# Spreading edge weights instead of messages, and running the last tiles' experts ahead of their gates: a fused graph layer on one Trainium2 core

## Chip, cores and metric

The kernel runs on 1 core of one Trainium2 chip. The metric is device time in microseconds (us) of that core, from start to end of one launch; lower is better.

## What is computed

A node layer over x of 6250 rows by 256: a graph attention over 200,000 edges, a linear attention, a sum, a norm, and then a mixture of four experts whose gates come from a second, small graph attention over 131,072 edges (edges to nodes past 6250 fall away). The change lies in this last part:

```python
h = (x_flat @ W_gat).reshape(M, HEADS, NUM_EXPERTS)              # 4 heads x 4 values a node
e = leaky_relu(a_src[src] + a_dst[dst], negative_slope=0.2)
alpha = softmax of e over the edges that share a dst
agg = segment_sum(h[src] * alpha[:, :, None], dst) + b_gat
scores = layernorm(agg).reshape(M, HEADS, NUM_EXPERTS).mean(1)
topk_s, topk_i = top_k(scores, 2);  w = softmax(topk_s)
for ei in range(4):
    g = where(topk_i == ei, w, 0.0).sum(-1)
    hh = gelu(x @ W1[ei] + b1[ei])
    out = out + g[..., None] * (hh @ W2[ei] + b2[ei])
```

The four experts can be computed without the gates; only the weighting and the sum need them.

## The kernel before

Nodes lie in 49 tiles of 128 (the last has 106). The first stage (first graph attention, linear attention, sorting of the second edge list) ends at about 2200 us of the profiled span, and the change leaves its work as it is, but for a few tiny operations in the check that sets `bad_2`. What matters starts there.

**Second edges.** The sorted edges are cut into 98 groups (`NGR`) of `G2` = 8 chunks of 128 edges, with some two groups to a tile of nodes. A group touches at most `W2` = 2 neighbouring tiles; `ohq` (128x8x2) says to which of the two an edge belongs. For each group, class `SecondEdges` has these steps, each a method:

- `gather` (L1303): 8 indirect DMAs on GpSimd (POOL), one for each chunk, which fetch each edge's source row from `htab` in DRAM. Six buffers, issued three groups ahead.
- `load` (L1319, SP queue), `one_hot_t` (L1332), `one_hot` (L1324): the one-hot matrices of the edges.
- `terms` (L1345, PE), `select` (L1353, L1357): the destination's factors, masked by `ohq`, summed to `pw`.
- `weights` (L1361, L1362): `pr = pw * gathered factors`, `wp = max`, 4 weights an edge. The first operation of DVE that needs the gather.
- `messages` (L1365 to L1377): `msg = values * wp` (160 elements a partition), split into three bf16 parts `m3` by four operations, and then `mq = m3 * ohq`, 960 bf16 elements, which puts each message into the columns of its tile and zeros into the other's.
- `add` (L1385 on PE, L1389, L1391 on DVE): one-hot times `mq`, summed over the group, added to `acc2`.

The intermediate `pw`, `wp` and `msg` lie in PSUM, in the tile `dv`.

**Gates.** `gates(w, lo, hi)` turns `acc2` of finished tiles into the gate of each expert: 33 short dependent steps on DVE (with one tanh on ACT). The list `GATES` says in which group's turn the gates of which tiles start; a step costs one `next()`, and up to `HOPS` = 7 are written out in each of three places of a group's turn.

**Experts.** `expert_steps` makes one list of 458 steps: for a pair (expert, block of `TT` = 4 tiles) a begin, 4 hidden steps (L1404 on PE, gelu on ACT at L1409) and one output step for each tile (L1422, L1424 on PE, then a `sink` on DVE). Experts 0 and 1 come first, ungated; they go to DRAM (`keep`, `early`). Then come experts 2 and 3, block by block (`total`): the sink of expert 2 multiplies the two early outputs, loaded back by `load_early`, by their gates and adds the node's row `kx` (L1497, L1498); both sinks add their own gated output straight from PSUM (L1499); the sink of expert 3 sends the tile out (L1501). So an output of experts 2 and 3 can't be used before its tile's gates are known.

**The order of the work** is written out by hand: one loop over the groups issues the methods above, and `experts(part)` writes out as many expert steps as a straight line from group 0 to group 98 asks for, but the last `REST` = 30, which come after the gates of tiles 44 to 48:

```python
experts_upto(FIRST + (3 * g + part) * (len(e_steps) - REST - FIRST) // (3 * NGR))
...
for _ in gates(w, GATED, NT):
    pass
experts_upto(len(e_steps))
```

Each engine works through its own instructions in order, and waits at the first one that isn't ready. A conditional block behind the loop (`bad != 0`) recomputes everything for edge lists that don't fit these assumptions.

Of the kernel before, what the change touches and what calls it, by code (L numbers as in the profile page):

```python
# [9 lines left out]
F32 = mybir.dt.float32  # L10
BF16 = mybir.dt.bfloat16
# [3 lines left out]
OP = mybir.AluOpType  # L15
AX = mybir.AxisListType
# [4 lines left out]
P = 128  # L21
# [11 lines left out]
G2 = 8  # L33
# [16 lines left out]


GB = 8
GATES = [(t, min(t + GB, 40), 2 * min(t + GB, 40) + 3) for t in range(0, 40, GB)] + [(40, 44, 91)]
GATED = 44


def rows(t):
    return min(P, N - t * P)
# [3 lines left out]
def gps_layer(ctx: ExitStack, tc: tile.TileContext, a: dict, out: bass.AP):  # L62
# [1157 lines left out]
    with tc.tile_pool(name="d_k", bufs=1) as dk:  # L1220
# [64 lines left out]
        class SecondEdges:  # L1285
# [4 lines left out]
            def __init__(self, w, gp, ps, dv, idx, dl, q, rows, eds, narrow=False):  # L1290
                self.w, self.gp, self.ps, self.eds, self.narrow = w, gp, ps, eds, narrow
                self.idx, self.dl, self.q, self.rows = idx, dl, q, rows
                self.lane = dv[:, 0:P]
                at = P
                for name, f in (("pw", 8), ("wp", 4), ("msg", HW)):
                    setattr(self, name, dv[:, at : at + G2 * f].rearrange("p (c f) -> p c f", f=f))
                    at += G2 * f

            def gather(self):
                self.gt = self.gp.tile([P, G2, HW + 8], F32, name="gt")  # L1300
# [49 lines left out]
            def select(self):  # L1350

                es = self.w.tile([P, G2, W2 * 3, 8], F32, name="e_sel", bufs=1)
                V.tensor_mul(  # L1353
                    es.rearrange("p c (q s) f -> p c q (s f)", q=W2), self.ed,
                    self.ohq[:, :, :, None].to_broadcast([P, G2, W2, 24]),
                )
                V.tensor_reduce(self.pw, es.rearrange("p c k f -> p c f k"), AX.X, OP.add)  # L1357

            def weights(self):
                pr = self.w.tile([P, G2, 8], F32, name="pr", bufs=1)  # L1360
                V.tensor_mul(pr, self.pw, self.gt[:, :, HW:])  # L1361
                V.tensor_max(self.wp, pr[:, :, 0:4], pr[:, :, 4:8])  # L1362

            def messages(self):
                V.tensor_mul(  # L1365
                    self.msg.rearrange("p c (h d) -> p c h d", h=4),
                    self.gt[:, :, 0:HW].rearrange("p c (h d) -> p c h d", h=4),
                    self.wp.unsqueeze(3).to_broadcast([P, G2, 4, 5]),
                )

                m3 = self.w.tile([P, G2, 3, HW], BF16, name="m3")
                V.tensor_copy(m3[:, :, 0], self.msg)
                V.tensor_sub(self.msg, self.msg, m3[:, :, 0])  # L1373
                V.tensor_copy(m3[:, :, 1], self.msg)
                V.tensor_sub(m3[:, :, 2], self.msg, m3[:, :, 1])
                self.mq = self.w.tile([P, G2, W2, 3 * HW], BF16, name="mq")
                V.tensor_mul(  # L1377
                    self.mq, m3.rearrange("p c s f -> p c (s f)")[:, :, None, :].to_broadcast([P, G2, W2, 3 * HW]),
                    self.ohq[:, :, :, None].to_broadcast([P, G2, W2, 3 * HW]),
                )  # L1380

            def add(self):
                ag = self.ps.tile([P, W2 * 3 * HW], F32, name="ag")
                for c in range(G2):
                    T.matmul(  # L1385
                        ag, self.oh[:, c], self.mq[:, c].rearrange("p q f -> p (q f)"), start=(c == 0), stop=(c == G2 - 1)
                    )
                part_ = self.w.tile([P, W2, HW], F32, name="ag3", bufs=1)
                V.tensor_reduce(part_, ag.rearrange("p (q s f) -> p q f s", q=W2, s=3), AX.X, OP.add)  # L1389
                at = acc2[:, ds(self.t, W2), :]  # L1390
                V.tensor_add(at, at, part_)  # L1391

# [87 lines left out]

        gated_to = 0

        def total(e, t0):


            def begin():
                if e == EARLY:
                    if t0 == 0:
                        load_early(0)
                    load_early(t0 + TT)  # L1490

            def sink(t, yo):
                assert t < gated_to
                n = rows(t)
                y = held[t0][:n, :, t - t0]
                if e == EARLY:
                    V.scalar_tensor_tensor(y[:, 0], y[:, 0], gate[:n, t, 0:1], kx[:n, t], op0=OP.mult, op1=OP.add)  # L1497
                    V.scalar_tensor_tensor(y[:, 0], y[:, 1], gate[:n, t, 1:2], y[:, 0], op0=OP.mult, op1=OP.add)  # L1498
                V.scalar_tensor_tensor(y[:, 0], yo[:n], gate[:n, t, e : e + 1], y[:, 0], op0=OP.mult, op1=OP.add)  # L1499
                if e == 3:  # L1500
                    SP.dma_start(out[t * P : t * P + n, :], y[:, 0])  # L1501

            return begin, sink

        def gates(w, lo, hi):

# [100 lines left out]
            yield  # L1607

        late = [(e, t0) for t0 in blocks for e in range(EARLY, 4)]
        e_steps = expert_steps([(e, t0) for e in range(EARLY) for t0 in blocks] + late, lambda e, t0: (keep if e < EARLY else total)(e, t0))  # L1610
        e_done = 0

        def experts_upto(k):
            nonlocal e_done
            for st_ in e_steps[e_done:k]:
                st_()
            e_done = max(e_done, k)

        with tc.tile_pool(name="g2_w", bufs=2) as w, tc.tile_pool(name="g2_g", bufs=6) as gp, tc.tile_pool(
# [9 lines left out]
                groups.append(SecondEdges(w, gp, ps, dv, src_2[:, cols], dl_2[:, cols], q_2[:, cols],  # L1629
                                          rows_2[g * G2 * P : (g + 1) * G2 * P, :], 2, g < NARROW))  # L1630
            AHEAD = 4
            REST = 30
            FIRST = 14
            in_turn = []
            HOPS = 7
            at_ = lambda i: groups[i].load()
            at_(0)
# [1 line left out]
            for g in range(-3, NGR + 1):  # L1639
                def at(i, stage):  # L1640
                    if 0 <= i < NGR:
                        getattr(groups[i], stage)()
                def experts(part):
                    if g < 0:
                        return experts_upto((3 * (g + 3) + part) * FIRST // 9)
                    for _ in range(HOPS):
                        if in_turn and next(in_turn[0], 0) == 0:
                            in_turn.pop(0)
                    experts_upto(FIRST + (3 * g + part) * (len(e_steps) - REST - FIRST) // (3 * NGR))
                if g == -3:  # L1650
                    for i in range(AHEAD):
                        at(i, "gather")
                elif g > 0:
                    at(g + AHEAD - 1, "gather")
                i = g + 3
                if 0 <= i < NGR and i % TL == 0:
                    _, ts_ = nc.values_load_multi_w_load_instructions(
                        t0_2[0:1, i : min(i + TL, NGR)], engines=(ENG.Activation, ENG.DVE), min_val=0, max_val=NT,
                        skip_runtime_bounds_check_because="the tiles are clamped",
                    )  # L1660
                    for j, t in enumerate(ts_):
                        groups[i + j].t = t
                in_turn += [gates(w, lo, hi) for lo, hi, g_ in GATES if g_ == g]
# [24 lines left out]
                experts(3)  # L1688
            for _ in gates(w, GATED, NT):
                pass  # L1690
            experts_upto(len(e_steps))
        with tc.If(bad != 0):

            own_edges()
# [26 lines left out]
            with tc.tile_pool(name="l_w", bufs=1) as w:  # L1721
                for lo in range(0, NT, GB):
                    for _ in gates(w, lo, min(lo + GB, NT)):
                        pass
            for st_ in expert_steps(late, total):
                st_()

# [27 lines left out]
```

## Time and profile before

| | |
|---|---|
| median of 3 runs | 3260.65 us (3256.18 to 3268.05) |
| the profiled execution's own time | 3258.8 us |
| its span, first to last instruction | 3257.0 us |
| granted clock of TensorE, mean | 0.857 |
| busy share PE, DVE, POOL, ACT | 72%, 75%, 72%, 15% |
| first and last gather of the second edges issued | 2200.41 us, 3202.68 us |
| last expert output leaves DVE | 3249.8 us |

A line of a group reads: line, engine, operation, output<-inputs, shapes and count, then busy time in all and the mean ns of one, then the idle time of the engine just before them and what ended most of it. A line of the timeline reads: start, duration, engine, line, operation, and in brackets the idle time of the engine before it. "issue" is time in which the engine waited for nothing that the profile shows. Instructions of one engine overlap at their ends, so the start of the next is a better measure of what one costs than its duration.

### The profile page before, as it was taken

To read this page: it belongs to the slowest core of one execution; us is meant where nothing else is said; L and a number is where in the kernel's file an instruction comes from. 1 tells how busy PE (TensorE), PEld (TensorE's weight loads), DVE (VectorE), ACT (ScalarE), POOL (GpSimd) and SP (SyncE) were. 2 spreads that over 40 slices of the span, in tenths; PEclk is the share of its full clock that TensorE was granted. 3 is DMA by queue.
4 is the path that set the end of the run, shared out by engine and by line. 5 is a ranking of instruction groups with operands and counts; after the bars stand their busy time and mean duration, and the time that the engine had idled before them with its cause. 6 is when DMAs were issued, how large, how long until landed. Compare 5 with 4: busy or idle time off the path is not lost. (4 is left out here: it accounts for less than half of the span.)

```text
span 3257.0 us, 36396 instructions
## 1 busy us (share of the span) xinstructions
PE 2334.0 (72%) x10899; PEld 1699.4 (52%) x10900; DVE 2439.4 (75%) x6337; ACT 480.6 (15%) x1266; POOL 2344.4 (72%) x2436
## 2 busy tenths in 40 slices
PE   7677778865666574665665666658777877888888
PEld 5555666654455453554544545445455545555555
DVE  7587767788888887886886878667676766777775
ACT  3200111111111111111111111013111111111111
POOL 2577777777777777777777777757777777777772
PEclk9788888987888887787888878779998998999989
DMA  6544444445555555555555555534223223333321
GB/s 202 155 135 135 136 129 127 137 134 145 150 139 151 143 137 140 138 141 143 141 153 142 147 140 142 138 92 101 61 62 78 60 57 92 81 76 80 78 51 37
DMA packets 248273, 384.90 MB, mean 118 GB/s; under 512 B 73414, under 2 KB 156246, under 8 KB 248057
## 3 DMA queue, kind: packets, MB, share of 16 engines
q0 software_dynamic: 103296, 230.96, 28.9%
q1 hardware_dynamic: 142857, 150.87, 15.4%
q8 instruction: 91, 1.49, 0.2%
q14 instruction: 125, 1.02, 0.1%
q10 hardware_dynamic: 1904, 0.56, 0.1%
HBM read 345.44 MB, written 36.74 MB: 117 GB/s over the span
## 5 line engine op out<-in xcount | busy, mean ns | idle before, releaser
L774 POOL DMA_INDIRECT gt<-ztab,src_c x1612 | 1551.2, 962 | 528.1 <-issue 424.7
L842 PE MATMUL ag<-gt,oh 128*128 128x260 f32 x3224 | 980.1, 461 | 348.3 <-DVE gt L833 347.0
L842 PEld LDWEIGHTS ag<-gt,oh 128*128 128x128 f32 x3224 | 732.6, 234 | 516.0 <-DVE gt L833 375.9
L1303 POOL DMA_INDIRECT gt<-htab,src x784 | 764.6, 975 | 262.5 <-issue 210.0
L833 DVE TENSOR_TENSOR gt<-gt,dv 128x1040 f32<-128x1040 f32 x403 | 488.8, 1223 | 0.2 <-DVE src L409 0.2
L1424 PE MATMUL yo<-w,hT 128*128 128x256 f32 x1568 | 420.8, 411 | 15.8 <-DVE ys L1467 15.8
L1404 PE MATMUL hp<-xy,w 128*128 128x512 f32 (+1 forms) x832 | 407.2, 612 | 8.6 <-ACT hT L1409 4.5
L1424 PEld LDWEIGHTS yo<-w,hT 128*128 128x128 f32 x1568 | 303.5, 203 | 96.1 <-issue 26.3
L208 DVE TENSOR_TENSOR src_d<-gt,most 128x32 f32<-128x32 f32 x204 | 38.6, 189 | 355.6 <-DMA gt<-ztab,src_c 344.3
L868 PE MATMUL m<-wqkv,xy 128*128 128x256 f32 (+1 forms) x784 | 235.8, 436 | 88.8 <-DVE kmax L879 43.6
L798 DVE TENSOR_TENSOR oh<-dv,dl_c 128x1024 f32<-128x1024 f32 x202 | 243.9, 1207 | 0.0
L868 PEld LDWEIGHTS m<-wqkv,xy 128*128 128x128 f32 (+1 forms) x784 | 160.7, 215 | 125.1 <-DVE kmax L879 49.6
L1404 PEld LDWEIGHTS hp<-xy,w 128*128 128x128 f32 x832 | 159.9, 205 | 112.4 <-issue 98.3
L1409 ACT ACTIVATE hT<-hp,b 128x512 f32<-128x512 f32 (+1 forms) x208 | 132.8, 660 | 517.6 <-PE hp L1404 294.9
L209 ACT ACTIVATE src_f<-src_d,shift_c 128x32 f32<-128x32 f32 x202 | 64.9, 321 | 928.2 <-DVE src_d L208 836.3
L1361 DVE TENSOR_TENSOR pr<-dv,gt 128x64 f32<-128x64 f32 x98 | 21.9, 223 | 227.0 <-DMA gt<-htab,src 219.5
L1385 PE MATMUL ag<-mq,oh 128*128 128x120 bf16 x784 | 66.3, 236 | 150.4 <-DVE mq L1377 141.0
L813 PE MATMUL ed<-pw,ohT 128*128 128x24 bf16 x1612 | 72.1, 175 | 125.5 <-DVE ohT L807 111.1
L373 DVE MAX8 src<-dl 128x8 f32<-128x1024 f32 x128 | 156.0, 1219 | 0.4 <-issue 0.4
L1385 PEld LDWEIGHTS <-oh 128*128 128x128 bf16 x784 | 51.6, 107 | 198.5 <-DVE mq L1377 176.6
L375 DVE MATCH_REPLACE8 dl<-src,dl 128x1024 f32<-128x1024 f32 x127 | 153.4, 1208 | 0.0
L813 PEld LDWEIGHTS <-ohT 128*128 128x128 bf16 x1612 | 64.0, 98 | 165.4 <-DVE ohT L807 134.3
(350 smaller groups left out, 2695.0 us busy)
## 6 DMA issues: line engine op xcount, KB each, us to landing
br<-rows SPq DMA_DIRECT2D x299, 256.0 KB
gt<-ztab,src_c POOLq DMA_INDIRECT x1612
gt<-htab,src POOLq DMA_INDIRECT x784
early<-ys SPq DMA_DIRECT2D x24, 512.0 KB
ys<-early SPq DMA_DIRECT2D x24, 512.0 KB
ztab<-zt SPq DMA_DIRECT2D x48, 132.0 KB
row<-in_x_dram SPq DMA_DIRECT2D x48, 128.0 KB
out_dram<-ys SPq DMA_DIRECT2D x48, 128.0 KB
```

Of the source, the lines that this page charges most:

```text
L373: V.max(out=srtf[:, 8 * i : 8 * i + 8], in_=keyf)
L375: V.match_replace(out=keyf, in_to_replace=srtf[:, 8 * i : 8 * i + 8], in_values=keyf, imm_value=0.0)
L774: G.indirect_dma_start(out=self.gt[:, c, :], out_offset=None, in_=ztab[:, :], in_offset=bass.IndirectOffsetOnAxis(ap=self.idx[:, c : c + 1 ...
L798: V.tensor_tensor(self.oh[:, :n], self.dv[:, None, :P].to_broadcast([P, n, P]), self.dl[:, :, None].to_broadcast([P, n, P]), op=OP.is_equal,)
L813: T.matmul(self.ed[:, c, :], self.ohT[:, c * P : (c + 1) * P], pw3[:, ds(self.tiles[c], 1), :].rearrange("p a b -> p (a b)"), start=True, ...
L833: V.tensor_mul(gz, gz, self.wp[:, c0:c1].unsqueeze(3).to_broadcast([P, c1 - c0, 4, 65]))
L842: T.matmul(sums[t], self.oh[:, c], self.gt[:, c, 0:ZW], start=(s0 + c == 0 or chunk_tile[s0 + c - 1] != t), stop=last,)
L868: T.matmul(out_, xy[:, t, j, :n], wqkv[:, j, c0 : c0 + D], start=(j == 0), stop=(j == 1))
L1303: G.indirect_dma_start(out=self.gt[:, c, : tab.shape[1]], out_offset=None, in_=tab[:, :], in_offset=bass.IndirectOffsetOnAxis(ap=self.idx[ ...
L1404: T.matmul(hp[:, :m], wts[e][0][:, c, j * P : (j + 1) * P], xy[:, t0 : t0 + nt, c] if m == nt * P else xy[:, t0, c, :m], start=(c == 0), s ...
L1409: S.activation(h[:, :m], hp[:, :m], AF.Gelu, bias=b1[:, e, j : j + 1])
L1424: T.matmul(yo[:n], hT[j][:, o : o + n], wts[e][1][:, j, :], start=(j == 0 and e < EARLY), stop=(j == 3))
```

## The change

1. `weights` multiplies the 4 weights of an edge by `ohq` into `wq` (8 chunks x 2 tiles x 4 heads = 64 elements); `messages` multiplies the gathered values by `wq` and so makes messages for both tiles at once (320 elements). The split into three bf16 parts runs over these 320 and writes `mq` directly; the product of 960 and the buffer `m3` are gone. `pw` and `wp` move from PSUM to SBUF.
2. For tiles 36 to 48 experts 2 and 3 run ungated, like experts 0 and 1: their outputs are copied by ACT (`hold`) into rows of `kx` that belong to tiles 0 to 25 and aren't needed any more. `total_held` puts gates and the four outputs together later.
3. `REST` is now a number of groups: all expert steps are written out by group 95. The gates are cut finer at the end (`GATED` = 46), and two steps of `total_held` run in each of the three places of a group's turn when no gate step is pending.
4. The first 26 tiles of `kx` are saved to DRAM (`rows_d`) by two DMAs in groups 4 and 8, for the conditional block.

```diff
-GATES = [(t, min(t + GB, 40), 2 * min(t + GB, 40) + 3) for t in range(0, 40, GB)] + [(40, 44, 91)]
-GATED = 44
+GATES = [(t0, t1, 2 * t1 + 3) for t0, t1 in [(0, 8), (8, 16), (16, 24), (24, 32), (32, 36), (36, 40), (40, 44), (44, 46)]]
+GATED = 46
+HELD = 36
...
+                self.pw = self.w.tile([P, G2, 8], F32, name="pw")
                 V.tensor_reduce(self.pw, es.rearrange("p c k f -> p c f k"), AX.X, OP.add)
             def weights(self):
...
-                V.tensor_max(self.wp, pr[:, :, 0:4], pr[:, :, 4:8])
+                wp = self.w.tile([P, G2, 4], F32, name="wp", bufs=1)
+                V.tensor_max(wp, pr[:, :, 0:4], pr[:, :, 4:8])
+                V.tensor_mul(
+                    self.wq, wp[:, :, None, :].to_broadcast([P, G2, W2, 4]),
+                    self.ohq[:, :, :, None].to_broadcast([P, G2, W2, 4]),
+                )
             def messages(self):
                 V.tensor_mul(
-                    self.msg.rearrange("p c (h d) -> p c h d", h=4),
-                    self.gt[:, :, 0:HW].rearrange("p c (h d) -> p c h d", h=4),
-                    self.wp.unsqueeze(3).to_broadcast([P, G2, 4, 5]),
+                    self.msg.rearrange("p c (q h d) -> p c q h d", q=W2, h=4),
+                    self.gt[:, :, 0:HW].rearrange("p c (h d) -> p c h d", h=4)[:, :, None].to_broadcast([P, G2, W2, 4, 5]),
+                    self.wq.unsqueeze(4).to_broadcast([P, G2, W2, 4, 5]),
                 )
-                m3 = self.w.tile([P, G2, 3, HW], BF16, name="m3")
-                V.tensor_copy(m3[:, :, 0], self.msg)
-                V.tensor_sub(self.msg, self.msg, m3[:, :, 0])
-                V.tensor_copy(m3[:, :, 1], self.msg)
-                V.tensor_sub(m3[:, :, 2], self.msg, m3[:, :, 1])
-                self.mq = self.w.tile([P, G2, W2, 3 * HW], BF16, name="mq")
-                V.tensor_mul(
-                    self.mq, m3.rearrange("p c s f -> p c (s f)")[:, :, None, :].to_broadcast([P, G2, W2, 3 * HW]),
-                    self.ohq[:, :, :, None].to_broadcast([P, G2, W2, 3 * HW]),
-                )
+                self.mq = self.w.tile([P, G2, 3, W2 * HW], BF16, name="mq")
+                V.tensor_copy(self.mq[:, :, 0], self.msg)
+                V.tensor_sub(self.msg, self.msg, self.mq[:, :, 0])
+                V.tensor_copy(self.mq[:, :, 1], self.msg)
+                V.tensor_sub(self.mq[:, :, 2], self.msg, self.mq[:, :, 1])
...
+        def hold(e, t0):
+            def sink(t, yo):
+                S.copy(kx[: rows(t), (e - EARLY) * NH + t - HELD], yo[: rows(t)])
+            return (lambda: None), sink
+        def add_early(t):
+            y = held[t - t % TT][:n, :, t % TT]
+            V.scalar_tensor_tensor(y[:, 0], y[:, 0], gate[:n, t, 0:1], kx[:n, t], op0=OP.mult, op1=OP.add)
+            yield
+            V.scalar_tensor_tensor(y[:, 0], y[:, 1], gate[:n, t, 1:2], y[:, 0], op0=OP.mult, op1=OP.add)
+            yield
+        def add_late(t, e, yo):
+            V.scalar_tensor_tensor(y, yo[:n], gate[:n, t, e : e + 1], y, op0=OP.mult, op1=OP.add)
+            if e == 3:
+                SP.dma_start(out[t * P : t * P + n, :], y)
...
+        def total_held(lo, hi):
+            for t in range(lo, hi):
+                if t % TT == 0:
+                    load_early(t)
+                yield from add_early(t)
+                for e in range(EARLY, 4):
+                    add_late(t, e, kx[:, (e - EARLY) * NH + t - HELD])
+                    yield
...
-            REST = 30
+            REST = 3
...
+                    for _ in range(2):
+                        if in_turn_2 and not in_turn and next(in_turn_2[0], 0) == 0:
+                            in_turn_2.pop(0)
-                    experts_upto(FIRST + (3 * g + part) * (len(e_steps) - REST - FIRST) // (3 * NGR))
+                    experts_upto(FIRST + (3 * g + part) * (len(e_steps) - FIRST) // (3 * (NGR - REST)))
...
+                if g in (4, 8):
+                    half = slice(0, NH) if g == 4 else slice(NH, 2 * NH)
+                    SP.dma_start(rows_d[:, half], kx[:, half])
...
-            for _ in gates(w, GATED, NT):
-                pass
-            experts_upto(len(e_steps))
+            for steps_ in (*in_turn, *in_turn_2, gates(w, GATED, NT), total_held(GATED, NT)):
+                for _ in steps_:
+                    pass
```

More of the change, by code (lines that the diff above doesn't have):

```diff
@@ L1293, in __init__ @@
                 self.lane = dv[:, 0:P]
[L1294 to L1297, printed above, removed]
+                at = P + G2 * W2 * 4
+                self.wq = dv[:, P:at].rearrange("p (c q h) -> p c q h", c=G2, q=W2)
+                self.msg = dv[:, at : at + G2 * W2 * HW].rearrange("p (c f) -> p c f", c=G2)
             def gather(self):
@@ L1385, in add @@
                     T.matmul(
-                        ag, self.oh[:, c], self.mq[:, c].rearrange("p q f -> p (q f)"), start=(c == 0), stop=(c == G2 - 1)
+                        ag, self.oh[:, c], self.mq[:, c].rearrange("p s f -> p (s f)"), start=(c == 0), stop=(c == G2 - 1)
                     )
                 part_ = self.w.tile([P, W2, HW], F32, name="ag3", bufs=1)
-                V.tensor_reduce(part_, ag.rearrange("p (q s f) -> p q f s", q=W2, s=3), AX.X, OP.add)
+                V.tensor_reduce(part_, ag.rearrange("p (s q f) -> p q f s", q=W2, s=3), AX.X, OP.add)
                 at = acc2[:, ds(self.t, W2), :]
@@ L1481, in gps_layer @@
         gated_to = 0
+        NH = NT - HELD
+        rows_d = dram.tile([P, 2 * NH, D], F32, name="rows_d")
+        def hold(e, t0):
[3 more added lines that the diff above has]
+        def add_early(t):
+            assert t < gated_to
+            n = rows(t)
+            y = held[t - t % TT][:n, :, t % TT]
[4 more added lines that the diff above has]
+        def add_late(t, e, yo):
+            n = rows(t)
+            y = held[t - t % TT][:n, 0, t % TT]
+            V.scalar_tensor_tensor(y, yo[:n], gate[:n, t, e : e + 1], y, op0=OP.mult, op1=OP.add)
+            if e == 3:
+                SP.dma_start(out[t * P : t * P + n, :], y)
         def total(e, t0):
@@ L1489, in begin @@
                         load_early(0)
-                    load_early(t0 + TT)
+                    if t0 + TT != HELD or again:
+                        load_early(t0 + TT)
             def sink(t, yo):
-                assert t < gated_to
-                n = rows(t)
-                y = held[t0][:n, :, t - t0]
                 if e == EARLY:
[L1497 to L1501, printed above, removed]
-            return begin, sink
+                    for _ in add_early(t):
+                        pass
+                add_late(t, e, yo)
+            return begin, sink
+        def total_held(lo, hi):
[6 more added lines that the diff above has]
+                    yield
+        again = False
         def gates(w, lo, hi):
@@ L1609, in gps_layer @@
         late = [(e, t0) for t0 in blocks for e in range(EARLY, 4)]
-        e_steps = expert_steps([(e, t0) for e in range(EARLY) for t0 in blocks] + late, lambda e, t0: (keep if e < EARLY else total)(e, t0))
+        e_steps = expert_steps([(e, t0) for e in range(EARLY) for t0 in blocks] + late, lambda e, t0: (keep if e < EARLY else total if t0 < HELD else hold)(e, t0))
         e_done = 0
@@ L1631, in gps_layer @@
             AHEAD = 4
-            REST = 30
+            REST = 3
             FIRST = 14
-            in_turn = []
+            in_turn, in_turn_2 = [], []
             HOPS = 7
@@ L1662, in gps_layer @@
                         groups[i + j].t = t
-                in_turn += [gates(w, lo, hi) for lo, hi, g_ in GATES if g_ == g]
+                for lo, hi, g_ in GATES:
+                    if g_ == g:
+                        in_turn.append(gates(w, lo, hi))
+                        if hi > HELD:
+                            in_turn_2.append(total_held(max(lo, HELD), hi))
+                if g in (4, 8):
+                    half = slice(0, NH) if g == 4 else slice(NH, 2 * NH)
+                    SP.dma_start(rows_d[:, half], kx[:, half])
                 at(g, "messages")
@@ L1688, in gps_layer @@
                 experts(3)
-            for _ in gates(w, GATED, NT):
-                pass
-            experts_upto(len(e_steps))
+            for steps_ in (*in_turn, *in_turn_2, gates(w, GATED, NT), total_held(GATED, NT)):
+                for _ in steps_:
+                    pass
         with tc.If(bad != 0):
@@ L1724, in gps_layer @@
                         pass
+            again = True
+            SP.dma_start(kx[:, : 2 * NH], rows_d)
             for st_ in expert_steps(late, total):
```

## The prediction

> **What bounds the kernel now.** I began with the page's chain that ended last and its groups, then went to the timeline of the stage with the second edges (from 2200 us).
>
> ```profile
> POOL 14%; DMA 6%; issue 5%; DVE 3%; PE 3%; ACT 0%; DVEq 0%; POOLq 0%; ACTq 0%
> ...
> L1303 POOL DMA_INDIRECT gt<-htab,src x784 | 764.6, 975 | 262.5 <-issue 210.0
> L1377 DVE TENSOR_TENSOR mq<-m,ohq 128x960 bf16<-128x960 bf16 x98 | 112.8, 1151 | 0.2 <-DVE pr L1361 0.2
> ```
>
> The chain lies mostly on POOL's gathers and the landing of the last one. The 784 gathers run from 2200.41 to 3203.63 us without a pause but the 0.3 us of "issue" between two: POOL sets the pace, 1003.2 / 98 = 10.24 us a group. The windows (length; busy and count of PE, PEld, DVE, ACT, POOL; granted clock; DMA share; GB/s) show the others with room there, and PE alone behind the last gather:
>
> ```profile
> 2800.00:2900.00 100.00, 82.99 (x394) 50.37 (x392) 70.20 (x183) 14.59 (x29) 76.53 (x78) 0.96 0.31 72
> ...
> 3200.00:3220.00 20.00, 16.43 (x61) 10.40 (x61) 11.19 (x36) 2.52 (x4) 2.83 (x3) 0.83 0.13 30
> 3220.00:3240.00 20.00, 19.55 (x81) 13.50 (x80) 11.55 (x43) 2.87 (x6) 0.00 (x0) 1.00 0.08 25
> ```
>
> The waits between 2250 and 3200 us tell whether PE and DVE could follow a faster POOL: PE stood idle for the messages, DVE for the gathers.
>
> ```profile
> DVE pr L1361 <- DMA gt<-htab,src: 214.9, 71, 7.5
> PE ag L1385 <- DVE mq L1377: 137.5, 57, 8.6
> ```
>
> The end, from the timeline: the last gather issues at 3202.68 us; its landing frees `pr`; the gates of tiles 44 to 48 begin; the last output leaves DVE. The span ends at 3257.0, so 7.2 us behind that are the store and the program's end, and 51.1 us lie between landing and end.
>
> ```profile
> 3202.68 0.95 POOL L1303 DMA_INDIRECT gt<-htab,src  x1 [0.31 <-issue]
> 3205.90 0.23 DVE L1361 TENSOR_TENSOR pr<-dv,gt 128x64 f32<-128x64 f32 x1 [4.61 <-DMA gt<-htab,src]
> 3216.36 0.18 DVE L1522 TENSOR_SCALAR ga_rd<-acc 128x20 f32<-128x20 f32 x1
> 3225.44 0.18 DVE L1605 TENSOR_TENSOR gate<-gate,ga_top 128x20 f32<-128x20 f32 x1
> 3249.34 0.48 DVE L1499 SCALAR_TENSOR_TENSOR ys<-yo,gate,ys 106x256 f32<-106x256 f32 x1 [2.98 <-PE yo L1424]
> ```
>
> **Part 1, weights instead of messages: what DVE saves.** Removed from each group: 322 + 312 + 324 + 318 + 317 (L1365 to L1375) + 1151 (L1377) = 2744 ns. In their place: five operations of 320 elements. Between L1365 (160 elements, 322 ns) and L1353 (384 elements, 548 ns), both with PSUM among their operands, an element costs 1.01 ns, so each takes about 484; `wq` has 64 elements like `pr` (L1361, 223). In all 2643 ns: 0.1 us less, 10 us over 98 groups, on an engine that waits 215 us for gathers. By itself worth nothing; POOL's waits hide it.
>
> **What POOL saves.** The timeline shows more:
>
> ```profile
> 2941.85 0.95 POOL L1303 DMA_INDIRECT gt<-htab,src  x1 [0.30 <-issue]
> 2942.41 1.15 DVE L1377 TENSOR_TENSOR mq<-m,ohq 128x960 bf16<-128x960 bf16 x1
> 2943.10 1.28 POOL L1303 DMA_INDIRECT gt<-htab,src  x1 [0.30 <-issue]
> 2944.68 0.94 POOL L1303 DMA_INDIRECT gt<-htab,src  x1 [0.30 <-issue]
> ```
>
> A gather takes 0.94 to 0.95 us (675 of the 781 that start from 2200 to 3200), but one that starts while L1377 runs takes longer by what is left of L1377 less some 0.13: here 2943.56 - 2943.10 = 0.46 left, 0.33 longer. Over these 781 the excess above 0.945 us sums to 24.5 us; 37 that start inside L1377 have 15.8 of it, 18 inside L1332 2.6, those inside L1497 and L1498 2.05. POOL is the pace, so L1377's 15.8 come off the end. What replaces it either reads one operand from PSUM (`msg` and `wq` lie in `dv`) or is as short as L1362, which reads two SBUF operands, takes 191 ns, and stretched a gather by only 0.03 us in all. The 26 new additions from SBUF (like L1497, 0.02 us each) cost 0.5. But the other operations shift against the gathers. Bounds: L1332's 0.48 us could meet a gather in each group (98 x 0.35 = 34 us, a loss of 16 net), or all 24.5 us vanish. I take 14.5, nearest to the row of L1377 itself.
>
> The Trainium skill ("SBUF — State Buffer", Who interferes with whom) speaks against this: a two-input `tensor_tensor` holds only the shared read interface, and descriptor generation, it infers, needs the write interface; so L1377 would not slow the gathers, and by that rule alone this term is 0 and the sum 3246.8. The same section says that two SBUF inputs do contend with a GpSimd instruction that reads SBUF, which would charge the three short new products. The 37 gathers decide for contention.
>
> **Part 2, experts ahead: the new tail.** Removed from behind the last gather: 30 expert steps, of which 12 are hidden and 11 outputs. At the pace of the timeline (hidden 3.43 us, 1.04 for the tile of 106; output 1.96) that is 4 x 3.43 + 8 x 1.04 + 11 x 1.96 = 43.6 us on PE, most of what ran from 3207 to 3249. It moves among the gathers. There PE's whole work at that pace was 721 us in 1003 us and becomes 765 in about 989: 7.8 us a group against 10.1. Its waits for `mq` (137 us) cover that; without the cover it would cost what rival C says. ACT's 26 copies (0.44 each, between L1334's 229 ns for 48 elements and L1409's 685 for 512) lie beside 85% idle time.
>
> Left behind the landing, on DVE alone and in order. In the order of writing, 12 gate steps of tiles 44 and 45 and all 8 additions of these tiles stand behind `pr` of group 97. By starts of neighbours: `pr`, last subtraction, max, `wq` 0.8; `one_hot` 1.1; gate steps 2.7; 8 additions of 0.4, 3.2; both groups' `add` 0.9; `messages` 2.1: 10.8 us (before: 10.5, with 2.0 of waiting for PE). Gates of 3 tiles instead of 5: 3225.62 - 3216.36 = 9.3 less the 0.4 of one interposed L1499 and some for shorter rows, 8.5. Tiles 46 and 47: 8 additions, 3.7. Tile 48: `load_early(48)` stands on SP's queue behind the store of tile 47, which waits for DVE; so DVE then waits for two loads: between 0 (landed before) and 6.5 us (the longest of the chain's landings), and I take 3.0, from the usual 2.3 of a gather plus two issues of 0.3. Four additions, 2.0. End, 7.2. Sum 35.2 against 51.1: 15.9 less. Bounds: 9 (load 6.5, no overlap of DVE operations) to 19 (load hidden).
>
> **What is added elsewhere.** Two more calls of `gates`, some 43 operations of about 0.2 us each: 17 us of DVE, in its 215 us of waiting. `load_early(36)` and `(40)` are no longer a block ahead: each waits some 5 us on DVE, with the next group's `pr` and PE's `mq` queued behind; POOL runs on, three groups ahead, and DVE catches up; 44's load has a group and a half to land. `rows_d`: 2 x 1.7 MB on SP's queue, 8 us each at the 202 GB/s of the page's first slice, 29 at the stage's 58. Behind it wait the `br` loads, needed two groups (20 us) later, and the gathers' landings; POOL doesn't stop for these. Uncovered, 2 x 9. For all of this I take 2 us, between 0 and 20.
>
> **Sum.** 3258.8 (own time) - 14.5 - 15.9 + 2 = 3230.4; the median of the runs lies 1.85 higher than the profiled execution, so 3232.
>
> **Rivals.** 0.5% is 16.3 us, about what a measurement of this kernel can tell from no change.
>
> A, the forecast: both parts pay, 3216 to 3246.
>
> B, the gathers don't get faster (L1332 or the additions land where L1377 did): only the tail, 3260.65 - 15.9 + 2 = 3247. For it: phases are locked to landings, and L1377 hit 37 of 98 groups. Against: the shorter operations leave less to wait for.
>
> B', the tail doesn't shrink (DVE late at the last landing, behind gate steps and early loads; loads at 6.5 us): 3260.65 - 14.5 - 0 to 5 = 3241 to 3246. Against: the windows show DVE at 70 to 77%.
>
> C, slower: PE becomes the bound. `add` of the last group stands on PE behind all expert steps, and gates and sums only start then. It decides where PE needs over 10.1 us a group; each 0.1 more is 9.8 us. For it: PE is 83% busy in the window shown, and its waits may be set by DVE's and ACT's turns rather than by spare time. If the 282 us without PE work were fixed, as a share, PE's stage would take 1003 x 765 / 721 = 1064 us, end 61 later than before, with 35 us behind it instead of 51: 3260.65 + 61 - 16 = 3306; half of that, 3283. Against: 137 us of waiting for `mq`, which comes with the gather.
>
> That the change fails to do what it says: PE steps still running after the last landing; that is C.
>
> **Numbers.** A 0.72, of which 0.04 above 3244; B 0.10; B' 0.08, half of it faster by over 0.5%; C 0.10. Faster 0.72, same 0.18, slower 0.10. The range reaches from A's low end to beyond B and leaves out C: 3215 to 3257.
>
> **What would show it.** Right: gathers of L1303 spaced 1.26 us instead of 1.280, last issue near 3188; mean duration from 975 ns to about 957; no L1404 or L1424 after it; last output some 21 us behind its landing plus the load; `PE ag <- DVE mq` well under 137. Wrong: the mean of L1303 at 975 or above (B), DVE waiting on `ys<-early` for over 5 us at the end (B'), or PE with no wait at `ag` and gathers landed long before `pr` (C).

## The result, and the profile after

The changed kernel takes 3229.85 us (median of 4 runs, 3226.18 to 3230.64) against 3263.59 us of the kernel before on the same chip (4 runs, 3256.18 to 3268.05): ratio 0.9893, 95% interval 0.9879 to 0.9907. The forecast was 3232 in 3215 to 3257. A later set of runs gave 3226.52 against 3264.14, ratio 0.9887, interval 0.9868 to 0.9907. The profiled execution of after took 3229.99 us, its span 3228.0. The medians differ by 33.7 us, the two profiled executions by 28.8 (3258.8 to 3229.99); what follows accounts for the latter.

The page of after, with its chain of what ended last and the row of the gathers:

```profile
POOL 14%; issue 6%; DMA 6%; DVE 4%; PE 2%; ACT 0%; DVEq 0%; POOLq 0%; ACTq 0%
...
L1303 POOL DMA_INDIRECT gt<-htab,src x784 | 748.5, 955 | 262.6 <-issue 210.3
```

The 784 gathers are 16.1 us of busy time shorter than before (764.6, 975 ns), their idle time is the same (262.5 before): they were not freed from a wait, each just takes less. The timeline gives a spacing of 1.2595 us instead of 1.2800. PE's share of the chain fell from 3 to 2%, DVE's rose.

The windows (columns as in the prediction), one amid the gathers and two at the end:

```profile
2800.00:2900.00 100.00, 87.13 (x408) 54.87 (x407) 74.29 (x194) 14.58 (x28) 76.21 (x79) 0.95 0.34 74
3180.00:3200.00 20.00, 1.97 (x16) 1.46 (x16) 10.63 (x43) 0.00 (x0) 8.49 (x9) 0.50 0.17 25
3200.00:3228.00 28.00, 0.98 (x8) 0.73 (x8) 20.52 (x95) 0.42 (x2) 0.00 (x0) 0.50 0.08 26
```

PE went from 83 to 87 in the first; at the end, where it had been at 16 to 20 of 20, it does almost nothing. The end belongs to DVE alone.

PE's and DVE's waits between 2250 and 3180 us (total, times, longest):

```profile
DVE pr L1362 <- DMA gt<-htab,src: 173.5, 54, 7.2
DVE pr L1362 <- issue: 68.1, 26, 5.8
...
PE yo L1426 <- DVE ys L1469: 50.2, 30, 5.0
PE yo L1424 <- DVE ys L1508: 32.1, 22, 4.4
PE ag L1387 <- DVE mq L1382: 27.0, 9, 8.7
```

PE's wait for `mq` fell from 134.7 in the same stretch of before to 27.0. Part of it went to two waits that were 16 and 2 us on PE before: an expert's output waits until DVE has emptied an earlier one (L1469 for experts 0 and 1, L1508 where gated outputs are added). DVE stood in front of both, and neither reached the gathers. DVE still stands at `pr` for 241.6 us (216.7 before, by the same two lines), so the gathers still set the pace.

The end, from the timeline:

```profile
3190.06 0.94 POOL L1303 DMA_INDIRECT gt<-htab,src  x1 [0.30 <-issue]
3193.58 0.23 DVE L1362 TENSOR_TENSOR pr<-pw,gt 128x64 f32<-128x64 f32 x1 [7.11 <-DMA gt<-htab,src]
3205.44 0.17 DVE L1559 TENSOR_SCALAR ga_rd<-acc 128x12 f32<-128x12 f32 x1
3216.58 0.17 DVE L1642 TENSOR_TENSOR gate<-gate,ga_top 128x12 f32<-128x12 f32 x1
3220.99 1.01 DVE L1508 SCALAR_TENSOR_TENSOR ys<-kx,gate,ys 106x256 f32<-106x256 f32 x2
```

Against before, `pr` of the last group starts 12.3 us earlier (3205.90), and from there to the end of the span it is 34.4 us instead of 51.1: 16.7 less. Together 29.0 us of span (3257.0 to 3228.0). The 7.11 us in the second line, in which DVE stands still with gate steps behind `pr` in its queue, are taken up below.

### The profile page after: what moved, and what is told of

The parts are those of the page before. It is cut to its first block, busy times and chain, and to the rows that moved or that the text cites. A ratio compares the mean times of both kernels' runs of the same rounds, so it can differ in the third digit from the quotient of the medians.

```text
span 3228.0 us, 36481 instructions
## 1 busy us (share of the span) xinstructions
PE 2300.0 (71%) x10899; PEld 1686.2 (52%) x10900; DVE 2434.3 (75%) x6425; ACT 487.9 (15%) x1294; POOL 2329.6 (72%) x2436
## 5 line engine op out<-in xcount | busy, mean ns | idle before, releaser
L1303 POOL DMA_INDIRECT gt<-htab,src x784 | 748.5, 955 | 262.6 <-issue 210.3
L1426 PE MATMUL yo<-w,hT 128*128 128x256 f32 x1568 | 409.9, 407 | 50.2 <-DVE ys L1469 50.2
L1406 PE MATMUL hp<-xy,w 128*128 128x512 f32 (+1 forms) x832 | 390.5, 594 | 9.7 <-ACT hT L1411 5.3
L1362 DVE TENSOR_TENSOR pr<-pw,gt 128x64 f32<-128x64 f32 x98 | 22.5, 230 | 251.2 <-DMA gt<-htab,src 180.6
L1324 DVE TENSOR_TENSOR oh<-dv,dl 128x1024 bf16<-128x1024 f32 x98 | 119.2, 1216 | 0.3
```

The source lines that it names most:

```text
L1303: G.indirect_dma_start(out=self.gt[:, c, : tab.shape[1]], out_offset=None, in_=tab[:, :], in_offset=bass.IndirectOffsetOnAxis(ap=self.idx[ ...
L1406: T.matmul(hp[:, :m], wts[e][0][:, c, j * P : (j + 1) * P], xy[:, t0 : t0 + nt, c] if m == nt * P else xy[:, t0, c, :m], start=(c == 0), s ...
L1426: T.matmul(yo[:n], hT[j][:, o : o + n], wts[e][1][:, j, :], start=(j == 0 and e < EARLY), stop=(j == 3))
```

## The experiments

The first eight runs fell on two chips on which the kernel before itself took 3963.12 and 3953.53 us, with POOL's share of the chain at 0 to 1%, so of those runs only traces and gathers are read here, and their totals for one thing at the end.

**1. What makes a gather longer: the engine's work, or where its operands lie?** The theory is that a DVE product of two operands in SBUF holds a gather that starts under it. The rival is that DVE's load as such, or the moment, does. Two kernels add the same useless product to each group of the changed kernel, with the second operand once from SBUF (`ohq`, as below) and once from PSUM (16 columns of `self.lane`, which lies in `dv`).

```diff
+                scr = self.w.tile([P, G2, W2, 3 * HW], BF16, name="scr", bufs=1)
+                V.tensor_mul(
+                    scr, self.mq.rearrange("p c s f -> p c (s f)").rearrange("p c (q f) -> p c q f", q=W2),
+                    self.ohq[:, :, :, None].to_broadcast([P, G2, W2, 3 * HW]),
+                )
```

> The changed kernel, and in each group one more DVE product of 128x960 bf16 into a scratch tile that nobody reads, both operands in SBUF, like the one that was removed. Theory (a product with two SBUF inputs holds up a gather that starts under it): mean gather back up by 10 to 30 ns, to 965 to 985 ns, the excess of gathers over 0.945 us, summed, up from 8 to between 16 and 32 us, and the time up by about as much, 8 to 24 us over the changed kernel. Rival (what counts is only how long DVE is busy): the same time as its twin with one operand in PSUM.

> The twin of the run with two SBUF inputs: the same additional product of 128x960 bf16 in each group, but its second operand is read from PSUM. Theory: mean gather stays at 953 to 958 ns, summed excess near 8 us, the time within 4 us of the changed kernel (DVE has the room for 1.1 us a group; the tail may carry two of them, 2 us). Rival (DVE's busy time counts): as slow as the run with two SBUF inputs.

Measured: two from SBUF, page and timeline:

```profile
L1303 POOL DMA_INDIRECT gt<-htab,src x784 | 785.0, 1001 | 492.0 <-issue 221.1
```

```profile
2763.23 1.15 DVE L1384 TENSOR_TENSOR scr<-mq,ohq 128x960 bf16<-128x960 bf16 x1
2763.27 1.92 POOL L1303 DMA_INDIRECT gt<-htab,src  x1 [0.30 <-issue]
```

One from PSUM, page and timeline:

```profile
L1303 POOL DMA_INDIRECT gt<-htab,src x784 | 746.2, 952 | 566.9 <-issue 210.7
```

```profile
2809.51 1.14 DVE L1384 TENSOR_TENSOR scr<-mq,dv 128x960 bf16<-128x960 bf16 x1
2809.52 0.94 POOL L1303 DMA_INDIRECT gt<-htab,src  x1 [0.30 <-issue]
```

The two products have the same shape and last equally long (median 1147 and 1144 ns). In the one kernel 68 gathers start while the product runs and lose 35.8 us above 0.945 us between them; in the other 69 do and lose nothing (their sum is within 0.2 of it). So it is the place of the second operand, not DVE's load; which part of a gather's issue is held, no run shows. The gather in the first timeline takes 0.98 us longer, and 1.11 us of the product were left when it started: again the remainder less 0.13. The totals, 3969.78 us (ratio to before 1.0004, 0.9973 to 1.0035) and 4010.85 (1.0097, 1.0062 to 1.0132) do not follow the gathers on that chip; the times that were expected did not come.

**2. The weights alone.** The kernel before with part 1 of the change and nothing else. Against the changed kernel:

```diff
-GATED = 46
-HELD = 36
+GATED = 44
...
-        def hold(e, t0):
...
-        def total_held(lo, hi):
...
-        e_steps = expert_steps(..., lambda e, t0: (keep if e < EARLY else total if t0 < HELD else hold)(e, t0))
+        e_steps = expert_steps(..., lambda e, t0: (keep if e < EARLY else total)(e, t0))
...
-            REST = 3
+            REST = 30
...
```

> The first part alone: weights are spread over the two tiles as in the changed kernel, but experts, gates and REST are as before. Theory (two separate gains: the long product with both operands in SBUF held up gathers, and PE's steps behind the last gather are a second, independent one): the mean gather falls from 975 to 955 ns, the last gather issues about 14 to 16 us earlier than before, the tail behind its landing stays near 51 us; 13 to 16 us faster than before, about 3247. Rival (the gathers' gain comes from the experts' new place, or from less waiting on DVE): mean gather stays at 970 to 975 ns and the time within 4 us of before.

> The kernel before with the new second edges alone (the experts of tiles 36 to 48 stay behind the last gather). On a chip where the kernel before takes about 3262 us: theory (the gathers win what the product with two SBUF operands held them by, and the tail stays as it was) 16 us less, 3246 (3242 to 3250), gathers at a mean of 953 to 957 ns, landing of the last group to the end 50 to 52 us. Rival (the gathers alone win nothing that reaches the end; all of the 33 us come from the tail): 3262 within 3 us. On the slower chip of the runs before this one, where the gathers wait for their buffers and do not set the pace: the mean of a gather falls as said and the time does not.

> The kernel before with the new second edges alone (the experts of tiles 36 to 48 stay behind the last gather). Theory where the kernel before takes about 3262 us: the gathers win what the product with two SBUF operands held them by and the tail stays as it was: 16 us less, 3246 (3242 to 3250); gathers at a mean of 953 to 957 ns, landing of the last group to the end 50 to 52 us. Rival (the faster gathers win nothing by themselves, the whole gain of the change is the tail's): 3262 within 3 us.

On the two slower chips the gathers' mean was 951 and 952 ns, totals 3997.17 us (1.0088, 1.0050 to 1.0125) and 3997.78 (1.0091, 1.0057 to 1.0125). The third run fell on a chip like that of the prediction: 3254.30 us (12 runs, 3249.81 to 3261.91) against 3260.92 of before, ratio 0.9985, interval 0.9975 to 0.9996. Some 5 to 7 us, so neither the 16 of the theory nor the rival's nothing. The gathers are nearly as fast as the theory has it (953 to 957 ns):

```profile
L1302 POOL DMA_INDIRECT gt<-htab,src x784 | 751.3, 958 | 262.4 <-issue 207.2
```

They are spaced 1.2631 us apart, and `pr` of the last group starts at 3190.70, 15.2 us ahead of before, of which 2.1 are an earlier start of the stage (2198.33 against 2200.41). But from there to the end it is 61.8 us instead of 51.1. The windows, and PE's timeline behind the last addition (its own, then the first and the last expert operation behind it) say why; the last fence has the last addition and the last expert operation of before:

```profile
3180.00:3200.00 20.00, 15.18 (x59) 9.39 (x59) 14.93 (x39) 2.73 (x4) 6.43 (x7) 0.91 0.17 38
3200.00:3220.00 20.00, 20.00 (x77) 12.22 (x76) 13.96 (x59) 3.54 (x6) 0.00 (x0) 1.00 0.10 35
3220.00:3240.00 20.00, 20.00 (x90) 14.79 (x89) 4.15 (x9) 3.01 (x7) 0.00 (x0) 1.00 0.07 24
```

```profile
3202.88 0.58 PE L1386 MATMUL ag<-mq,oh 128*128 128x120 bf16 x8
3203.40 0.28 PE L1423 MATMUL yo<-b,ones 3*128 3x256 bf16 x1
...
3243.09 1.89 PE L1425 MATMUL yo<-w,hT 128*106 128x256 f32 x8
```

```profile
3215.18 0.58 PE L1385 MATMUL ag<-mq,oh 128*128 128x120 bf16 x8
...
3247.41 1.89 PE L1424 MATMUL yo<-w,hT 128*106 128x256 f32 x8
```

PE works without a pause from 3193.06 to 3244.98: its list of expert steps sets the end, as it did in the kernel before. PE's last operation ends 4.3 us earlier than there (3249.30 to 3244.98), 2.1 of them by the earlier start of the stage; the spans differ by 4.5 (3257.0 and 3252.5). Two things kept it from more. From 2250 to 3180 us PE's waits went from 165.0 us in sum over its lines to 158.7, only 6.3 less: the wait for `mq` fell from 134.7 to 74.6, but the waits until DVE has emptied an earlier output rose from 17.7 to 60.5.

And more work stands behind the last addition: 13 outputs and 14 hidden steps, where before had 10 and three quarters of another and 12. This is not a matter of timing. PE takes its steps in the same order in all three runs of this kernel, on three chips, so that order is fixed in the built program; it is not that of the kernel before, though the source writes the expert steps in the same places. From the last addition to PE's last operation it is 42.1 us instead of 34.1, which is 8.0 of the 10.7 us by which the tail grew. So this run differs from before in two things, the gathers' time and the order of PE's steps, and what faster gathers would bring in the old order was not run.

What it shows is that an earlier landing does not reach the end as long as PE's list ends last. Part 2 takes that list off the end, and in the changed kernel the earlier landing reaches it.

**3. The experts ahead alone.** The changed kernel with the old second edges. Against the changed kernel:

```diff
-                self.mq = self.w.tile([P, G2, 3, W2 * HW], BF16, name="mq")
...
+                m3 = self.w.tile([P, G2, 3, HW], BF16, name="m3")
...
+                V.tensor_mul(
+                    self.mq, m3.rearrange("p c s f -> p c (s f)")[:, :, None, :].to_broadcast([P, G2, W2, 3 * HW]),
+                    self.ohq[:, :, :, None].to_broadcast([P, G2, W2, 3 * HW]),
+                )
```

> The second part alone: experts 2 and 3 of tiles 36 to 48 ahead of their gates, but messages are spread by the old long product with both operands in SBUF. Theory: mean gather stays at 970 to 975 ns, the landing of the last gather stays near 3206 us, the tail shrinks from 51 to 33 to 36 us; 14 to 18 us faster than before, about 3246. Rival (the tail shrinks only because gathers end earlier or DVE has less to do): under 8 us faster. If the two parts add up, the gains of this and of the run with weights only sum to the whole change's 30 to 34 us.

> The changed kernel with the old second edges (experts of tiles 36 to 48 ahead alone). Chip where the kernel before takes about 3262 us: theory (the tail is 16.7 us shorter, the stage starts some 3 us later, the gathers keep their 975 ns) 13 to 17 us less, 3247 (3243 to 3251); landing of the last group to the end 33 to 37 us. Rival (the two parts only pay together, since PE's added work among the gathers is covered only while messages come earlier): 3255 or more, with gathers starting late.

Both runs were on the slower chips: 3964.39 us (0.9995, 0.9966 to 1.0024) and 3962.35 (1.0035, 1.0006 to 1.0063), the gathers' mean back at 987 and 992 ns with the product (in the second, 74 gathers start under it alone and lose 31.4 us). What part 2 brings by itself on a chip like that of the prediction was not measured, so whether the two parts add up is not shown.

**4. How far PE is from being the bound (rival C).** Two useless matmuls more in each group of the changed kernel.

```diff
+                for r_ in range(2):
+                    T.matmul(
+                        ag_all[:, W2 * 3 * HW :], xy[:, r_, 0, :],
+                        xy[:, 0:2].rearrange("p t j n -> p (t j n)")[:, : 512 - W2 * 3 * HW], start=True, stop=True,
...
+                    )
```

> The changed kernel with two idle matmuls more (128x392, f32, some 2.6 us of PE together) in every group behind those of its addition; their results are not used. It looks for the point from which the prediction's rival C decides. Theory (PE needs 7.8 us a group by the prediction's count and 10.06 are there; 10.4 is just over): PE becomes the bound, and the end moves out by 98 times what it is over, 0.34 us, so 33 us more than the changed kernel (20 to 60, as gathers and messages cannot be met without any waiting). Rival one (the count of PE is too high, there is more room): under 10 us more. Rival two (PE's idle time was never spare, the full load comes on top): 98 x 2.6 = 255 us more.

> The changed kernel with two idle matmuls more (128x392, f32, some 2.6 us of PE together) in every group behind those of its addition; their results are not used. It looks for the point from which rival C decides. Theory (PE needs 7.8 us a group by the prediction's count and 10.06 are there; 10.4 is just over): PE becomes the bound, and the end moves out by 98 times 0.34 us, 33 us more than the changed kernel's 3226 to 3230, so some 3261 (3247 to 3290, as gathers and messages cannot be met without any waiting). Rival one (the count of PE is too high, there is more room): under 10 us more. Rival two (PE's idle time was never spare, the full load comes on top): 98 x 2.6 = 255 us more.

The first, on a slower chip: 3996.13 us (1.0109, 1.0057 to 1.0161), the gathers 952 ns. The second: 3225.57 us (4 runs, 3223.79 to 3232.20), ratio to before 0.9904, interval 0.9888 to 0.9921, which is the changed kernel's own. Rival one of the expectation holds: no change. A window, and PE's longest wait and its wait for `mq` from 2250 to 3180 us:

```profile
2800.00:2900.00 100.00, 100.00 (x471) 61.14 (x470) 75.82 (x190) 16.76 (x32) 75.62 (x81) 1.00 0.32 75
```

```profile
PE yo L1433 <- DVE ys L1476: 21.3, 20, 3.4
...
PE ag L1388 <- DVE mq L1382: 1.5, 2, 1.1
```

PE is busy for all of these 100 us, and the gathers are spaced 1.2593 us as ever. The added matmuls took 1.55 us a group by their rows (147.6 us in 95 groups), not the 2.6 expected; from 2800 to 3180 us PE was busy for 373.82 of 380, which is 9.91 us of a group's 10.07, after 8.82 (332.66) in the changed kernel. So the added work went into PE's waits down to the last tenths. It ends just short of the point from which rival C decides, and what lies beyond was not run.

**5. A shorter tail.** In after, the gate steps and additions of tiles 44 and 45 stand on DVE behind `pr` of the last group, though they need nothing of it, and DVE stands still for 7.11 us before `pr`. This kernel writes them out first at the last turn but one, and orders `weights` behind `add` of the group before and behind the last of these additions.

```diff
-                at(g + 1, "weights")
+                if g < 0:
+                    at(g + 1, "weights")
...
+                if g == NGR - 2:
+                    for steps_ in (*in_turn, *in_turn_2):
+                        for _ in steps_:
+                            pass
+                    in_turn, in_turn_2 = [], []
+                if 0 <= g < NGR - 1:
+                    with tc.issue_after(groups[g].last.ins), tc.issue_after(last_op.ins) if g == NGR - 2 else nullcontext():
+                        at(g + 1, "weights")
```

> The changed kernel with the weights of a group put at the end of the turn before it, and at the last turn all gate steps and additions of tiles 44 and 45 ahead of the weights of the last group, so that VectorE does them in its 7 us of waiting for the last gather and not behind it. Theory (some 28 gate steps and 8 additions stood behind the landing without need, and they are on the path): 8 to 10 us less than the changed kernel, on a chip where that takes 3230 us some 3221; last landing to the end 25 to 28 us instead of 34.4. Rival (the order of those steps costs as much ahead of the last gathers as it saves behind: buffers come free later, the last gathers are issued later): within 3 us of the changed kernel.

> The changed kernel itself, beside the reordered tail on the same chip. Theory where the kernel before takes about 3262 us: 3229 (3225 to 3233), gathers at a mean of 955 ns, 34 us from the last landing to the end. On a slower chip, where engines stand still with nothing to wait for that the profile shows and the gathers do not set the pace: within 1.5% of the kernel before on either side, with the gathers' mean at 952 to 957 ns all the same. Rival there (the saving of the tail survives since VectorE alone makes it): 15 us or more under the kernel before.

> The changed kernel with the weights of a group at the end of the turn before it, and at the last turn all gate steps and additions of tiles 44 and 45 ahead of the weights of the last group. Theory where the changed kernel takes 3229 us: 8 to 10 us less, some 3220; last landing to the end 25 to 28 us instead of 34.4. Rival (done ahead of the last gathers the steps hold the buffers of these back as long): within 3 us of the changed kernel. On a slower chip: the tail shorter as said, the total not told apart.

The first, on a slower chip: 3984.64 us (1.0092, 1.0061 to 1.0123). The other two, changed kernel and reordered one on one chip: 3226.52 us (3221.72 to 3232.12) and 3222.52 (3219.04 to 3224.53), ratios to before 0.9887 and 0.9876 (0.9859 to 0.9892). So 4 us less where 8 to 10 were expected, with intervals that overlap. It is the fastest kernel of this study by its median, but four runs of each do not separate it from the changed kernel. The timeline of the reordered tail:

```profile
3188.53 0.94 POOL L1303 DMA_INDIRECT gt<-htab,src  x1 [0.30 <-issue]
...
3192.74 0.22 DVE L1362 TENSOR_TENSOR pr<-pw,gt 128x64 f32<-128x64 f32 x1
3197.72 0.17 DVE L1562 TENSOR_SCALAR ga_rd<-acc 128x12 f32<-128x12 f32 x1
3205.83 0.17 DVE L1645 TENSOR_TENSOR gate<-gate,ga_top 128x12 f32<-128x12 f32 x1
```

`pr` to the end is 24.5 us (3217.2 - 3192.74); in the changed kernel on that chip it was 34.4. The tail itself gave the 9.9 us asked of it. Some was lost ahead of it: the gathers start 1.5 us later (2201.11 against 2199.62, within what the first stage varies by: 2198.3 to 2203.9 in the profiles of this study), take 1.1 longer in all, and `pr` now starts 4.21 us behind the issue of the last gather instead of 3.47, with no idle time before it, since DVE is still at the additions. 9.9 - 1.5 - 1.1 - 0.7 = 6.6, the difference of the two spans (3223.8 and 3217.2).

## Why the prediction was right, point by point

- **What POOL saves, 14.5 us.** Measured 16.1 in busy time, and as much in the stage's length (first to last gather, 1002.3 to 986.2 us). Of the 24.5 us of excess 8.4 are left: some 2 under L1332 and some 4 under the additions L1500, L1502 and L1508; the short products with two SBUF operands, which were to be small, are small (0.4 us under L1362). By the trace of before 61 gathers start under L1377 and 44 of them are lengthened, where the prediction counted 37; the 15.8 us stand. So nothing landed in the product's place, and rival B did not happen. The Trainium skill's "SBUF — State Buffer" (Who interferes with whom) infers that a `tensor_tensor` does not hold descriptor generation; here 35.8 us against none, with operands in SBUF and with one in PSUM, speak against it.
- **That these us come off the end.** Right in this change, wrong as it was argued. "POOL is the pace, so L1377's 15.8 come off the end" leaves out PE's list: in the run of the weights alone, 15.2 us earlier at the landing became 4.5 at the end (spans 3257.0 and 3252.5), as PE's list, which the build had made 8.0 us longer behind the last addition, set the end.
- **The tail, 35.2 us.** Measured 34.4, by terms that missed both ways. `pr` to the end of the gates was put at 10.8 + 8.5 = 19.3 and took 23.2, as `pr` of the last group came ahead of `messages` of the one before in DVE's order. So two `messages` stood behind it (4.0 us instead of 2.1) and two `one_hot` (2.3 instead of 1.1), and of the gate steps of tiles 44 and 45 28 instead of 12 (all gate steps together 12.4 us instead of 11.2). Additions 3.2 instead of 3.7; the wait for `load_early(48)` 0 instead of 3.0 (issued at 3181.83, long before it was needed); the last four additions 2.0 as said; the end 6.0 instead of 7.2. That the sum is off by 0.8 only is luck.
- **What is added elsewhere, 2 us.** Nothing that can be seen: POOL's idle time is 262.6 against 262.5 us, and no two gathers lie over 2 us apart.
- **Rival C.** The count of PE, 7.8 us a group, was too low: the windows give 8.82. The moved list was put too high instead: 43.6 us at 3.43 and 1.04 a hidden step. In the tail of before a hidden step takes 1.82 from start to start (four rows of 128x512) and 0.53 for the tile of 106, and the list 34.1. PE's room was real all the same: 1.1 us more of busy time a group was taken without a trace of it at the end, because PE's waits were spare time (126.5 us in all from 2250 to 3180 us, 35.0 with the two matmuls more). The clock helped too, see below.
- **What was to be seen.** Spacing 1.26 (1.2595), mean 957 ns (955), last issue near 3188 (3190.06, of which 3.45 is a later start of the stage), no L1404 or L1424 of the experts behind it (PE 1.97 and 0.98 us in the last two windows), `PE ag <- DVE mq` well under 137 (27.0). The last output "some 21 us behind its landing plus the load" was a slip: the terms of the sum make 25.0 and the load's 3.0, and 28.4 was measured (3222.0 - 3193.58), with no wait for the load.

## What to carry to other kernels

Before a stage's gain is taken off the end, look at what ends last behind that stage: if another engine has a list of work there, the gain reaches the end only as far as that list ends earlier (here 4.5 us of span with PE's list behind the landing, 29.0 with the list moved). Compare the order of each engine's instructions too before a difference is put down to time: an edit for one engine can change the order that the build gives another. Two kernels that differ in one operand's place tell whether an engine is slowed by another's load or by where the operands lie. An engine that stands still at a wait for a late transfer should find the work that needs nothing of it ahead of that wait in its queue; it is worth reading an engine's order at the last turn for that.

## What the runs showed of the hardware

**TensorE's clock pays for part of added work.** With the two matmuls more, the granted clock from 2800 to 3180 us was 1.00, against 0.96 and 0.94 in the two profiles of the changed kernel; over the span it was 0.868 or 0.869 in all four runs, against 0.853 to 0.860 in the eight runs of the changed kernel. The mean of an expert matmul (128x256) fell from 407 ns to 391. 41 us of busy time were added there for the 58 us that the new rows took at 1.55 us a group. Where PE did almost nothing, at the end of after, the clock shown is 0.50.

**Slower chips, and an effect that stays open.** On the two chips with 3963 and 3954 us, the mean granted clock of the kernel before was 0.78 to 0.79 (0.85 to 0.86 elsewhere), and engines stood still with no cause that the profile names. The chain of the kernel with the operand in PSUM:

```profile
PE 13%; another core or an unknown queue 9%; DVE 7%; issue 3%; ACT 1%; POOL 0%; DMA 0%; DVEq 0%; ACTq 0%; POOLq 0%
```

PE there issued matmuls of one output 0.7 and 1.4 us apart for over 6 us on end (3310.71 to 3317.02 us in the second run of the weights alone), where 0.2 us apart is usual. And the order of the kernels turned round: the three runs with a product of two SBUF operands in each group had ratios of 0.9995 to 1.0035, the five without it 1.0088 to 1.0109, though their gathers were 35 to 50 ns faster. Why faster gathers go with a slower program there was not found. Which of the two kernels of this case is faster on such a chip was not measured.
